# Four heads a step in the first mLSTM cell, and the second cell beside attention: a four-layer fp32 kernel on one Trainium2 core

## The chip, the cores and the metric

The kernel runs on one core of one Trainium2 chip. The metric is the device time of one execution in microseconds, the median over several runs. All arithmetic that matters here is in fp32.

## What is computed

Eight sequences b of 512 tokens and 256 features pass through four residual layers. The change touches the first layer and the entry to the second.

```python
x = x + tanh(g_xattn[0]) * mLSTM(layernorm(x), ctx, ctx)     # cell, 8 heads of 32
x = x + tanh(g_ffn[0])   * L0_ffn(layernorm(x))              # 32 heads of 8, then experts
x = x + tanh(g_xattn[1]) * cross_attention(ctx, ctx, layernorm(x))   # 16 heads of 16
x = x + tanh(g_ffn[1])   * key_value_memory(layernorm(x))

# mLSTM of one sequence, q = layernorm(x), k = v = ctx
log_f = log_sigmoid(fg); cs = cumsum(log_f)
log_D = where(causal, cs[:, None] - cs[None, :], -inf) + ig[None, :]
D = exp(log_D - max(log_D, -1))
C = (q k^T / sqrt(32)) * D
h = C / (max(|sum C|, exp(-max log_D)) + 1e-6) @ v
return layernorm(h) * ln_scale

# L0_ffn starts with a layer norm of its own: xn = layernorm(layernorm(x)) * ln_g + ln_b
```

## The kernel before

**Stages.** One long phase (`attention_phase`) holds the first three layers for all eight sequences; two shorter phases do the last layer. Sequences are taken in the order 0, 4, 1, 5, 2, 6, 3, 7 and numbered m = 0 to 7 in it. The backbone of the long phase is a list of 24 attention jobs: A(m, 0) and A(m, 1), the two halves of the heads of the second layer, and C(m, 0), the cross attention. Each job has 16 steps, each of two halves. Attention makes two passes: `maxima` (L397) multiplies queries with keys (L388, TensorE) and takes row maxima (L406, VectorE); after a job's last step `close_maxima` (L412) writes the maxima into the query operand; `exponentials` (L426) multiplies again and exponentiates (L434, ScalarE), and `values` (L440) sums with the values (L449). The two passes of neighbouring jobs run in the same steps: while one job exponentiates, the next one takes maxima.

**Work beside attention.** All else is written as Python generators, called lanes (L1147 to L1149): `before` runs `cell` and `queries`; `between` spreads operands and marks jobs ready; `behind` runs the experts and the operands of the cross attention; `after` and `fill` lead to the last layer. A lane yields a number, the TensorE time in rough microseconds that it has just used, or a tuple: `("wait", t)` asks not to be called before planned time t has gone by, `("rest", key)` waits for a key, `("take", on)` takes or gives back one PSUM bank that lanes share. After each half step `beside` (L1152) calls lanes until a credit of 1.1 or 2.1 units is used up. TensorE executes in exactly that written order; the order of the other engines is settled by a scheduler from the order of writing. A tick is one turn of the main loop (L1177): one step of the maxima of one job, of the exponentials of another, or both. Where no job is ready, ticks go by with lanes alone.

**The cell (L586 to L750), before.** For one sequence: x and the context are loaded by GpSimd's queue (L589, L497, L592), x is normalised, transposed to features (L313), and multiplied with the gate weights (L606). Gate functions on 8 partitions follow (L611 to L631), and the row of negated maxima goes to DRAM (L633), from where each of four pairs of heads reads it as a broadcast (L654). For a pair and each of four chunks of 128 keys: GpSimd masks the triangle (L662), ScalarE makes the decay of both heads (L670), TensorE the scores (L699), VectorE their product (L704), TensorE the sums with the keys (L677, 64 columns a head). Chunk c covers the queries from 128c on, so it has 512, 384, 256 or 128 columns. After the chunks the sums are transposed and divided (L715 to L737). At the end the result is normalised, scaled and added to x (L742 to L748).

**Two places for cells.** Class `Tiles` (L518) has buffers of its own; class `Lent` (L545) has its in those of the experts' weights, which come into use later. Sequences 0, 2, 4, 5, 6, 7 go through `Tiles`, 1 and 3 through `Lent`. Both lanes begin at once, so cells 0 and 1 run together ahead of attention. `queries` (L753) takes two layer norms one after the other (L755, L756), transposes, and projects to queries, keys and values through DRAM. `begin` (L801) spreads them over the attention operands: three sets `qa`, `ka`, filled by GpSimd at the start (L275, L276) and given rows of ones by SP (L284). The loop also holds back the exponentials of any job until the values of sequence 1 are made (L1189). `behind` waits for the end of the `Lent` lane.

## Time and profile before

| what | value |
|---|---|
| median of 3 runs | 3959.41 us (3946.13 to 3970.28) |
| the profiled execution | 3974.63 us, its span 3972.8 us |
| TensorE (PE) busy | 3616.3 us, 91% of the span |
| VectorE (DVE), ScalarE (ACT), GpSimd (POOL) busy | 57%, 44%, 16% |
| mean granted TensorE clock | 0.949 of full speed |
| maxima of the first job A(0, 0), L406 | 195.6 to 313.5 us |
| exponentials, L434, first and last | 327.7 us, 3054.3 us |

The profiled execution is one run, and 15 us longer than the median. Times in the profile count from the start of its span. A line such as `L388 PE MATMUL sc<-ka,qa` names the code line, the engine, the operation, and the tiles written and read. PE is TensorE's matmul row and PEld its weight loads; a busy PE is not PE at its peak. In the timeline an arrow in brackets names what ended the idle time of the engine before the instruction. The granted clock is that of TensorE alone. Each fp32 matmul appears as two instructions in the counts.

### The profile page before, as it was taken

The page shows a single profiled execution, that of the slowest core. Times are in us where ns is not written, and L with a number is a line of the kernel's source. Part 1 is how long each engine was busy: PE and PEld are TensorE (multiplying, and loading weights), DVE is VectorE, ACT ScalarE, POOL GpSimd, SP SyncE. Part 2 cuts the span into 40 slices and gives each one's busy share as a digit, 9 for nine tenths or more (in the row PEclk, how much of TensorE's full clock was granted, in tenths as well). Part 3 has the DMA queues.
Part 4 walks back from the last instruction along what each step waited for, and adds up shares of the span by engine and source line. Part 5 has one row for each costly group of instructions (what it writes and reads, how often), then busy time and mean ns, then how long its engine had stood idle before and what let it go on. Part 6 is the DMA issues. An engine that isn't in the chain of part 4 may idle for free.

```text
span 3972.8 us, 76203 instructions
## 1 busy us (share of the span) xinstructions
PE 3616.3 (91%) x31049; PEld 1861.4 (47%) x31049; DVE 2277.6 (57%) x5591; ACT 1763.3 (44%) x2305; POOL 617.2 (16%) x653
## 2 busy tenths in 40 slices
PE   5788889888899999999989988988899899999998
PEld 2332334333334433444434433434344677777776
DVE  4465665656555555554454453454421589999993
ACT  2213444454445445444444444434244355555552
POOL 3301121103001200200100010010000133333331
PEclk7567999999999999999999999999899999999999
DMA  3221221213222421333323223120333443333331
GB/s 95 93 74 38 72 73 58 86 39 81 77 73 76 117 75 57 100 95 91 95 80 105 80 64 97 60 71 25 120 107 120 112 130 103 104 103 112 111 108 36
DMA packets 221754, 339.05 MB, mean 85 GB/s; under 512 B 25998, under 2 KB 170926, under 8 KB 213102
## 3 DMA queue, kind: packets, MB, share of 16 engines
q1 hardware_dynamic: 203772, 273.04, 23.0%
q0 software_dynamic: 16768, 60.83, 5.3%
q8 instruction: 244, 4.00, 0.4%
q14 instruction: 106, 0.87, 0.1%
q10 hardware_dynamic: 864, 0.32, 0.0%
HBM read 236.66 MB, written 96.63 MB: 84 GB/s over the span
## 4 chain that ended last, share of the span: by engine, by line
PE 63%; DVE 8%; DMA 1%; ACT 1%; issue 1%; POOL 0%; SPq 0%; DVEq 0%; ACTq 0%; POOLq 0%
PE sc L388 17%; PE acc L1563 11%; PE ps_hd L131 10%; DVE nm L406 6%; PE av L449 5%; PE cf L1543 3%; PE ps_sim L1295 3%; PE ps_y L870 2%; PE ps_q L348 2%; PE ps_h L851 2%; PE ps_p L337 2%; PE ps_hl L131 1%; PE ps_g L964 1%; PE ps_t L318 1%; PE ot L470 1%
## 5 line engine op out<-in xcount | busy, mean ns | idle before, releaser
L406 DVE TENSOR_REDUCE nm<-sc 128x2 f32<-128x1024 f32 x768 | 940.4, 1225 | 1049.0 <-PE sc L388 1048.3
L434 ACT ACTIVATE pr<-sc 128x1024 f32<-128x1024 f32 x768 | 786.1, 1024 | 1009.9 <-PE sc L388 1009.4
L388 PE MATMUL sc<-ka,qa 32*128 32x512 f32 x3072 | 958.8, 673 | 162.5 <-DVE nm L406 141.4
L388 PE MATMUL sc<-qa,ka 32*128 32x512 f32 x3072 | 898.7, 658 | 19.4 <-ACT pr L434 17.1
L388 PEld LDWEIGHTS sc<-ka,qa 32*128 32x128 f32 x3072 | 260.6, 191 | 557.8 <-DVE nm L406 345.2
L1563 PE MATMUL acc<-up_sb,gs 64*128 64x256 f32 x4096 | 468.4, 382 | 1.3 <-DVE gs L1552 1.3
L131 PE MATMUL ps_hd<-xT,dw 128*64 128x256 f32 x3584 | 432.7, 387 | 9.1 <-DVE pd L704 5.0
L449 PE MATMUL av<-pr,v 128*32 128x512 f32 x3072 | 422.4, 623 | 1.1 <-ACT pr L434 1.1
L1563 PEld LDWEIGHTS acc<-up_sb,gs 64*128 64x128 f32 x4096 | 390.0, 187 | 52.3 <-issue 4.7
L131 PEld LDWEIGHTS ps_hd<-xT,dw 128*64 128x64 f32 x3584 | 243.6, 137 | 231.5 <-issue 100.9
L1533 POOL TENSOR_TENSOR m<-o,cwT 128x1024 f32<-128x1024 bf16 x128 | 243.7, 1904 | 562.9 <-DVE o L1531 240.7
L388 PEld LDWEIGHTS sc<-qa,ka 32*128 32x128 f32 x3072 | 242.5, 187 | 69.8 <-ACT pr L434 42.5
L1030 ACT COPY hb<-ps_hd 128x512 f32<-128x512 f32 x224 | 131.1, 586 | 307.8 <-PE ps_hd L131 283.6
L670 ACT ACTIVATE pd<-mb,aT 128x512 f32<-128x512 f32 (+3 forms) x256 | 128.9, 553 | 171.8 <-PE cav L677 89.0
L449 PEld LDWEIGHTS av<-pr,v 128*32 128x32 f32 x3072 | 61.4, 109 | 305.3 <-issue 289.7
L1552 DVE TENSOR_TENSOR gs<-cf,gs 128x1024 f32<-128x1024 f32 x128 | 155.6, 1217 | 42.2 <-PE cf L1543 27.4
L699 PE MATMUL csc<-qT,cT 32*128 32x384 f32 (+3 forms) x512 | 143.4, 580 | 13.8 <-DVE pd L704 7.4
L662 POOL TENSOR_SCALAR_AFFINE_SELECT mb<-mb 128x256 f32<-128x256 f32 x128 | 52.3, 409 | 653.3 <-ACT pd L670 370.6
L1543 PE MATMUL cf<-m,m 64*64 64x64 f32 x8192 | 152.4, 221 | 0.8 <-DVE gs L1552 0.7
L1543 PEld LDWEIGHTS cf<-m,m 64*64 64x64 f32 x8192 | 134.8, 135 | 38.7 <-issue 38.3
L704 DVE SCALAR_TENSOR_TENSOR pd<-csc,pd 128x512 f32<-128x512 f32 (+3 forms) x256 | 114.6, 483 | 66.4 <-PE csc L699 46.2
L1529 ACT CAST m<-o 128x1024 f32<-128x1024 bf16 x128 | 133.6, 1044 | 39.5 <-DVE o L1527 35.7
(232 smaller groups left out, 4134.6 us busy)
## 6 DMA issues: line engine op xcount, KB each, us to landing
h_d<-hb SPq DMA_DIRECT2D x224, 256.0 KB
gs<-h_d SPq DMA_DIRECT2D x56, 1024.0 KB
dw<-in_down SPq DMA_DIRECT2D x112, 256.0 KB
mb<-nM_d SPq DMA_DIRECT2D x32, 512.0 KB
qk_d<-pk SPq DMA_DIRECT2D x64, 256.0 KB
w1e<-in_w POOLq DMA_DIRECT2D x16, 1024.0 KB, 5.5
w2e<-in_w POOLq DMA_DIRECT2D x16, 1024.0 KB, 6.6
ws<-in_w SPq DMA_DIRECT2D x56, 256.0 KB
```

The lines of the kernel that those rows point to most:

```text
L131: nc.tensor.matmul(ps[64 * q : 64 * q + 64, :], dw[:, k, :], runs[:, :, q, :], start=(k == 0), stop=(k == NK - 1),)
L388: nc.tensor.matmul(sc[:, i, :], lhs[r : r + 32, g, c * P : (c + 1) * P], rhs[r : r + 32, g, :], start=True, stop=True,)
L406: newest = nc.vector.tensor_reduce(self.nm[:, c, 2 * half : 2 * half + 2, g], sc, AX.X, ALU.max, negate=True)
L434: nc.scalar.activation(self.pr[jj], sc, AF.Exp)
L449: nc.tensor.matmul(self.av[32 * j : 32 * j + 32, :], self.va[:, c, h * (self.hd + 1) : h * (self.hd + 1) + 32], pr[j // 2][:, j % 2, :], s ...
L699: nc.tensor.matmul(sc[i][:, s0:], cT[r : r + 32, g, s0 : s0 + P], qT[r : r + 32, g, s0:], start=True, stop=True,)
L1030: nc.scalar.copy(hb.rearrange("p n i t -> p i n t"), ps.rearrange("p i (n t) -> p i n t", n=2),)
L1529: nc.scalar.copy(m1, o1)
L1533: nc.gpsimd.tensor_tensor(m2, o2, tokens(cw), ALU.mult)
L1543: nc.tensor.matmul(cf[64 * q : 64 * q + 64, h, s, :], m2[rows, 4 * q + s // 2, :, s % 2], m1[rows, 4 * q + s // 2, :, s % 2], start=True, ...
L1552: nc.vector.tensor_tensor(gv, cf.rearrange("p h s i -> p i h s"), gv, ALU.mult)
L1563: nc.tensor.matmul(accs[n][q], gs[n % 2][rows, i, :], up_sb[rows, i, :], start=(i == 0), stop=(i == 63),)
```

## The change

- **Start.** x of the first sequence is loaded first, in two halves on SP's and ScalarE's queues, then its context and keys on SP's. GpSimd fills one set of attention operands at the start; `begin` has the other two filled when they are first wanted. The product of the output bias and the transposed mask (`constants`) come after the first cell's gate products.
- **First cell.** `all_pairs` does four heads in each of eight steps. Its broadcast rows lie in set 1 of the attention operands, half of its decays in set 2, its score products in the banks of the attention's scores. The decays run two steps ahead, the sums one step behind.
- **Its end.** The result's layer norm, scale and residual become two VectorE calls per chunk.
- **Layer norm of a layer norm.** For every sequence `queries` takes one statistic. With variance v it multiplies by 1/sqrt((1 + eps) v + eps^2), which is both norms in one.
- **Second cell.** `Tiles` takes sequences 0, 1, 3, 4, 5, 6, 7 and `Lent` takes 2 alone; it starts when the first attention job has started. The exponentials are not held for sequence 1 any more, and cells always share the one bank.

The diff, cut to its core; `close` holds what stood at L715 to L737.

```diff
-        for c in range(NC):
+        for c in range(NC) if dst is not None else ():
...
+        x0 = trp.tile([P, NC, D], F32, name="qn", tag="t1")
+        for c2 in range(2):
+            part = slice(2 * c2, 2 * c2 + 2)
+            (nc.sync, nc.scalar)[c2].dma_start(
+                x0[:, part], x[order[0]].rearrange("(c p) d -> p c d", p=P)[:, part]
+            )
...
+        cT0 = cxp.tile([P, NK, S], F32, name="cT", tag="cTc")
+        nc.sync.dma_start(cT0, cxT[order[0]].rearrange("(k p) s -> p k s", p=P))
+        cte = cst.tile([P, NC, WC], F32, name="cte")
+        nc.gpsimd.memset(cte, 1.0)
+        def load_keys(eng, ce, b):
+            for c in range(NC):
+                eng.dma_start(
+                    ce[:, c, : 8 * 33].rearrange("p (h e) -> p h e", e=33)[:, :, 0:32],
+                    cx[b, c * P : (c + 1) * P].rearrange("p (h e) -> p h e", e=32),
+                )
+        load_keys(nc.sync, cte, order[0])
...
+        def prepare(i):
+            qa, ka = sets[i]
             nc.gpsimd.memset(qa, 1.0)
             nc.gpsimd.memset(ka, 0.0)
-            sets.append((qa, ka))
+            if i:
+                give_ones(ka)
+        def give_ones(ka):
+            for j in range(4):
+                nc.sync.dma_start(
+                    ka[32 * j + 17 : 32 * j + 18, :, :], ones_d.rearrange("(o g) s -> o g s", o=1)
+                )
+        prepare(0)
         ones_d = drm.tile([4, S], F32, name="ones_d", bufs=1)
...
+        def constants():
...
+            def begin(self, m):
+                b = order[m]
+                if m == 0:
+                    return x0, cT0, cte
+                qn = self.tokens("qn")
+                nc.gpsimd.dma_start(qn, x[b].rearrange("(c p) d -> p c d", p=P))
+                cT, ce = self.context(m)
+                load_keys(nc.gpsimd, ce, b)
+                return qn, cT, ce
...
+        def all_pairs(qT, cT, ce, nM_d, aT, close):
+            room = [t[:, 2 * i : 2 * i + 2] for t in sets[1] for i in range(2)]
+            for pair in range(4):
+                nc.sync.dma_start(
+                    room[pair], nM_d[2 * pair : 2 * pair + 2].partition_broadcast(P)
+                )
+            spare = [t[:, 2 * i : 2 * i + 2] for t in sets[2] for i in range(2)]
+            pds, avs = {}, {}
+            steps = [(g, c) for g in range(2) for c in range(NC)]
+            def decay(n):
+                g, c = steps[n]
+                s0 = c * P
+                for pair in (2 * g, 2 * g + 1):
+                    mb = room[pair]
+                    nc.gpsimd.affine_select(
+                        out=mb[:, :, s0 : s0 + P], in_=mb[:, :, s0 : s0 + P],
+                        pattern=[[0, 2], [1, P]], compare_op=ALU.is_ge,
+                        fill=NEG, base=0, channel_multiplier=-1,
+                    )
+                    pd = pds[pair, c] = (
+                        spare[c - 1 + pair % 2] if c % 2
+                        else prb.tile([P, 2, S], F32, name="pr", tag="pr")
+                    )
+                    for i in range(2):
+                        h = 2 * pair + i
+                        nc.scalar.activation(
+                            pd[:, i, s0:], mb[:, i, s0:], AF.Exp, bias=aT[:, c, h : h + 1]
+                        )
+            def weigh(n):
+                g, c = steps[n]
+                s0 = c * P
+                two = {
+                    pair: ps_sc.tile([P, 2, S], F32, name="sc", tag="sc")
+                    for pair in (2 * g, 2 * g + 1)
+                }
+                for pair, sc in two.items():
+                    for i in range(2):
+                        r = 32 * (2 * (pair % 2) + i)
+                        nc.tensor.matmul(
+                            sc[:, i, s0:], cT[r : r + 32, g, s0 : s0 + P], qT[r : r + 32, g, s0:],
+                            start=True, stop=True,
+                        )
+                for pair, sc in two.items():
+                    pd = pds[pair, c]
+                    nc.vector.scalar_tensor_tensor(
+                        pd[:, :, s0:], sc[:, :, s0:], 1.0 / math.sqrt(32.0), pd[:, :, s0:],
+                        ALU.mult, ALU.mult,
+                    )
+            def sums(n):
+                g, c = steps[n]
+                for pair in (2 * g, 2 * g + 1):
+                    if c == 0:
+                        avs[pair] = (
+                            ps_av.tile([P, S], F32, name="av", tag="av") if pair % 2
+                            else ps_ac.tile([P, S], F32, name="cav", tag="ac")
+                        )
+                    for i in range(2):
+                        h = 2 * pair + i
+                        nc.tensor.matmul(
+                            avs[pair][64 * i : 64 * i + 64, c * P :],
+                            ce[:, c, 33 * h : 33 * h + 64],
+                            pds[pair, c][:, i, c * P :], start=(c == 0), stop=(c == NC - 1),
+                        )
+            decay(0)
+            decay(1)
+            for n in range(len(steps) + 1):
+                if n < len(steps):
+                    weigh(n)
+                if n > 0:
+                    sums(n - 1)
+                    g, c = steps[n - 1]
+                    if c == NC - 1:
+                        for pair in (2 * g, 2 * g + 1):
+                            close(pair, avs[pair])
+                if n + 2 < len(steps):
+                    decay(n + 2)
...
-            qn = own.tokens("qn")
-            nc.gpsimd.dma_start(qn, x[b].rearrange("(c p) d -> p c d", p=P))
-            cT, ce = own.context(m)
-            for c in range(NC):
-                nc.gpsimd.dma_start(
-                    ce[:, c, : 8 * 33].rearrange("p (h e) -> p h e", e=33)[:, :, 0:32],
-                    cx[b, c * P : (c + 1) * P].rearrange("p (h e) -> p h e", e=32),
-                )
+            qn, cT, ce = own.begin(m)
             yield ("wait", 4)
...
+            if m == 0:
+                constants()
...
+            def close(pair, av):
+                avs = trp.tile([P, S], F32, name="avs", tag="pk", bufs=2)
+                nc.any.tensor_copy(avs, av)
...
+            if m == 0:
+                all_pairs(qT, cT, ce, nM_d, aT, close)
+            for pair in range(4) if m else ():
...
-                def banks():
-                    if newest:
-                        return [ps_m.tile([P, S], F32, name="csc", tag="m") for _ in range(2)]
-                    two = ps_sc.tile([P, 2, S], F32, name="csc2", tag="sc")
-                    return [two[:, i] for i in range(2)]
...
+            if m == 0:
+                mu, rs = yield from layernorm(None, hk, "q")
+                for c in range(NC):
+                    nc.vector.scalar_tensor_tensor(
+                        hk[:, c, :], hk[:, c, :], mu[:, c, 0:1], lns, ALU.subtract, ALU.mult
+                    )
+                    nc.vector.scalar_tensor_tensor(
+                        Xa[:, c, :], hk[:, c, :], rs[:, c : c + 1], Xa[:, c, :], ALU.mult, ALU.add
+                    )
+            else:
+                yield from layernorm(hk, hk, "q" + own.user)
+                nc.gpsimd.tensor_tensor(
+                    hk, hk, lns.unsqueeze(1).to_broadcast([P, NC, D]), ALU.mult
+                )
+                nc.gpsimd.tensor_tensor(Xa, Xa, hk, ALU.add)
             xds[m] = drm.tile([P, NC, D], F32, name="x_d1", bufs=M)
...
-            lnx[m] = yield from layernorm(xn, Xa, "q" + own.user, kept=m)
-            yield from layernorm(xn, xn, "q" + own.user)
+            mu, rs = lnx[m] = yield from layernorm(None, Xa, "q" + own.user, kept=m)
+            both = small.tile([P, NC], F32, name="rs2", tag=f"rs2{own.user}", bufs=1)
+            nc.gpsimd.tensor_scalar(
+                both, mu[:, :, 1], 1.0 + EPS_LN, EPS_LN * EPS_LN, ALU.mult, ALU.add
+            )
+            nc.gpsimd.tensor_tensor(both, both, mhalf.to_broadcast([P, NC]), ALU.pow)
+            yield ("wait", 2)
+            for c in range(NC):
+                nc.vector.tensor_scalar(
+                    xn[:, c, :], Xa[:, c, :], mu[:, c, 0:1], both[:, c : c + 1],
+                    ALU.subtract, ALU.mult,
+                )
+                if c % 2:
+                    yield ("wait", 1.5)
...
+                if last is None and i:
+                    prepare(i)
...
+                if m == f == 0:
+                    yield ("wait", 6)
...
+            if tiles is Lent:
+                yield ("rest", ("begun", 0))
...
-        lanes += [Lane(before((0, 2, *range(4, M)), Tiles)), Lane(behind()), Lane(before((1, 3), Lent))]
+        lanes += [Lane(before((0, 1, *range(3, M)), Tiles)), Lane(behind()), Lane(before((2,), Lent))]
...
-                    or not free or ("v_d", 1) not in rested
+                    or not free
...
+                rested.add(("begun", 0))
```

## The prediction

> **What bounds the kernel now.** I read the page's slices first.
>
> ```profile
> PE   5788889888899999999989988988899899999998
> ...
> PEclk7567999999999999999999999999899999999999
> ```
>
> TensorE is at 8 or 9 tenths from the third slice (99 us each) to the end, at full clock from the fifth. What is left lies at the start: idle time, and a clock of 0.5 to 0.7 over four slices. Next, busy time by stretch (columns: length, then PE, PEld, DVE, ACT, POOL with counts, granted clock, DMA share, GB/s), and the matmuls of the maxima and the exponentials in the first 400 us.
>
> ```profile
> 0.00:60.00 60.00, 19.33 (x61) 9.07 (x61) 31.80 (x56) 12.54 (x17) 32.80 (x43) 0.90 0.44 116
> 60.00:192.60 132.60, 99.59 (x328) 43.16 (x328) 57.84 (x167) 36.64 (x75) 41.15 (x65) 0.54 0.28 88
> 192.60:327.00 134.40, 119.62 (x335) 44.88 (x338) 74.60 (x124) 27.12 (x50) 10.93 (x25) 0.61 0.22 56
> ...
> 800.70:921.30 120.60, 108.96 (x661) 46.66 (x664) 69.60 (x110) 61.01 (x77) 8.82 (x17) 0.99 0.16 43
> 921.30:1022.60 101.30, 86.22 (x540) 36.17 (x536) 63.86 (x116) 42.28 (x49) 30.64 (x36) 0.97 0.32 88
> ```
>
> ```profile
> L388 PE MATMUL sc<-ka,qa x204: 587/1056/1217, 192.7 to 397.2; 32*128 32x512 f32 x102
> ...
> L434 ACT ACTIVATE pr<-sc x17: 999/1024/1025, 327.7 to 397.9; 128x1024 f32<-128x1024 f32 x17
> ```
>
> No attention matmul runs before 192.7 us; the first exponential comes at 327.7. Until then two cells run together. Last, the timeline of that start (start, length, engine):
>
> ```profile
> 3.92 11.25 DVE L213 COPY gwm<-gw_sb 128x16 f32<-128x16 f32 x1 [2.92 <-DMA gw_sb<-in_gw]
> ...
> 20.39 1.41 DVE L98 BATCH_NORM_STATS2 ln_st<-qn 128x6 f32<-128x256 f32 x4 [3.90 <-DMA qn<-in_x]
> ...
> 31.86 0.73 DVE L107 TENSOR_SCALAR qn<-qn,ln_mv,ln_rs 128x256 f32<-128x256 f32 x2 [2.23 <-POOL ln_rs L104]
> ...
> 56.45 1.31 SPq L633 DMA_DIRECT2D nM_d<-pd  x2
> ...
> 62.08 0.42 POOL L662 TENSOR_SCALAR_AFFINE_SELECT mb<-mb 128x256 f32<-128x256 f32 x1 [23.14 <-DMA mb<-nM_d]
> ...
> 97.32 3.36 PE L699 MATMUL csc<-qT,cT 32*128 32x512 f32 x8
> ...
> 100.61 2.15 PE L677 MATMUL cav<-pd,cte 128*64 128x512 f32 x4
> ...
> 149.95 0.32 SPq L748 DMA_DIRECT2D x_d<-Xa  x1
> ...
> 171.90 0.73 DVE L107 TENSOR_SCALAR xn<-xn,ln_mv,ln_rs 128x256 f32<-128x256 f32 x2 [0.58 <-POOL ln_rs L104]
> ```
>
> The chain of cell 0 is latency up to 62 us, matmul at half clock to about 140, and layer norms and projections from there to 192.7.
>
> **What the Trainium skill says.** "SBUF — State Buffer", Who interferes with whom: a VectorE copy in a two-port mode and a GpSimd instruction share a port pair that one holds whole while the other blocks. The trace agrees: a 16-element copy lasts 11.25 us, from 3.92 until the GpSimd fills end at 15.1, and everything on VectorE queues behind it. "TensorE: Matmul & The Clock Gate", Part 1: the clock is at half after an idle window and at full after a busy one. The trace agrees on the two values, yet shows 0.54 over 60 to 192.6 although PE is busy 99.6 of 132.6 us; so I price the start at both clocks. Same page, Part 3: matmuls of 32 rows in four different row groups run side by side. The attention products here use it; the old cell used two groups.
>
> **The change, part by part: the path to the first maximum.**
>
> Loads and fills. x goes out first on SP's and ACT's queues, and nothing of the second cell. It should land by about 6 us, but VectorE is held by the GpSimd fills until those end: ident 0.5, gwm 0.24, cell keys 1.08, one set of attention operands instead of three (2 x 1.80), v0 1.25, v1 1.05: 7.7 from 0.7, so 8.5. Statistics 1.41 and 0.36, rs on GpSimd about 1.5 with its hand-overs: the first normalised chunk at 12.2 instead of 31.9. GpSimd no longer issues 2 x 5.3 us of loads ahead of rs. SP gets about seven more issues of 0.4 us and a wait for the key fill ahead of the weights, which are wanted 80 us later: no cost. I allow 8 to 16.
>
> Gates. From first chunk to the row of maxima took 24.6 us (31.9 to 56.45) for two cells interleaved. Without the other cell's gate matmuls (3.4) and its exponents and scans in between (about 3) it is 18: 30 (28 to 34). The moved constants (bo product 2.1 us of PE, 1.2 of VectorE) lie under ScalarE's gate functions; at worst 1 us. Write and broadcast took 5.6 (56.45 to 62.08): 36. Four broadcasts of 512 KB now compete, so up to 4 more.
>
> All pairs. Per group of four heads at half clock: scores side by side 2.08, 1.65, 1.22, 0.80 by chunk, 5.75; sums 2.15, 1.55, 1.12, 0.70 per pair, 11.0 for two; transposes 2.2. Two groups: 38. At full clock 19. ScalarE needs 2 x 4 x (0.66 + 0.56 + 0.46 + 0.35) = 16.3, VectorE 12.8 (one call per pair for two; the old calls of 0.65, 0.53, 0.41, 0.28 would make 15, one start of 0.16 less each, about 12.8) plus 4.8 of divisions: 17.6. With 8 of lead-in and last division: 46 at half clock; at full clock about 30, as steps alternate between PE and VectorE. I take 38: 74.
>
> Norms. The cell's own norm and residual took 10 us (139.9 to 149.95), with two GpSimd calls of 2.34 each. Now statistics 1.8, rs 1.5, eight VectorE calls of about 0.45: 7. The double norm took 22 (149.95 to 171.9); now one statistic, four small GpSimd calls (2 x 0.23 + 2 x 1.04) and hand-overs: 4. From the normalised chunk to the first maximum 20.8 (171.9 to 192.7), unchanged. 74 + 7 + 4 + 20.8 = 106. **Gain 192.7 - 106 = 87** (bounds 53 with everything late at 140, 103 at 90).
>
> **What comes back.** Cell 1 now runs beside attention. Its yields add up to 2.2 (features) + 3.6 (gates) + 0.8 + 4 x 6.325 (pairs) = 31.9 units, in a planner that hands out 1.1 + 2.1 = 3.2 a tick. Counting lanes tick by tick by the code's own yields, old and new order both take 412 ticks from the first maximum to the last sum; the loop does 29 units more, nearly all in ticks that had spare credit (job A(2,0) 43 units for 33, A(5,1) 52 for 43, A(6,1) 35 for 26). A unit's price: the job of 800.7 carries 52 units and takes 120.6 us, that of 921.3 carries 29 and takes 101.3: 0.84; against the job of 693.6 (33 units, 107.1 us) 0.71. 29 x 0.75 = **22 us** (15 if spare time hides half, 32 at 1 us a unit).
>
> Cell 1's operands are ready at tick 29 by that count, wanted at 32: no stall, margin three ticks. The fills of sets 1 and 2 (7.2 us of GpSimd) and their eight small stores move behind the first maximum; their jobs start 16 and 32 ticks later, so nothing waits; at worst 4 us if they get ahead of a store on SP, which all stores of the features share. The double norm saves 3.5 us of VectorE per sequence; VectorE is at 57%: nothing. The dropped test on the second cell's values bound nothing: it was done at 269, the exponentials began at 327.7. The first 32 ticks keep their length: maxima plus about as much beside them (43 and 34 units for 42 and 44).
>
> **Sum.** -87 + 22 = -65. The profiled execution took 3974.6 (span 3972.8 plus 1.8), so its like would take 3910; it lies 15 above the median 3959.4, and against that I predict **3895**.
>
> **Rivals.** *A slow start* (chance 0.15): PE stays at half clock, broadcasts queue, VectorE is held longer; so that its early x gains little; the first maximum at 140. For it: 0.54 granted, and the 43 us that GpSimd waited for broadcasts. Against: nothing is queued beside cell 0 now. 3959 - 53 + 22 = 3928. *The work of cell 1 is free* (0.12): spare credit and idle PE time hide it and the start runs at full clock; first maximum at 95, 5 us back: 3959 - 98 + 5 = 3866. *PE blocks behind the cells* (0.05): PE keeps its program order, so a score or sum of cells 1 and 2 that waits for GpSimd, ScalarE and VectorE holds the attention products behind it. There are 2 x 4 x 4 = 32 such chunks in the first 32 ticks; the gain of 65 is gone at 2.0 us each, and at 3.0 the result is 3959 - 65 + 96 = 3990. Against: cells 2 and 3 stood in the same place before, and PE was busy 119.6 of 134.4 us.
>
> **Numbers.** The forecast 0.68. Differences under 0.5% (20 us) cannot be told from no change here. Range: from the lowest own case (first maximum 90, 15 back: 3871) and the free case 3866 less some scatter, to the slow start plus scatter: 3856 to 3938. Faster by over 0.5%: the forecast, the free case and most of the slow start, 0.89; within 0.06; slower 0.05.
>
> **What would show it.** First maximum at 100 to 112 us, first exponential 130 to 140 after it, first broadcast select near 36, eight-matmul score steps, maxima of A(1,0) directly behind A(0,1), last exponential near 2990. Wrong if the first maximum is after 130, if A(1,0) stalls, or if the attention stretch (2728 us from first to last exponential) grows by over 35.

## The result

The changed kernel takes 3934.7 us (median of 12 runs, 3929.6 to 3947.3) where the kernel before, beside it on the same chips, takes 3967.6: the ratio is 0.9931, with a 95% interval of 0.9914 to 0.9949. It is 33 us faster. The forecast was a change of 65; the time lies inside the stated range, but half of the expected gain is missing. The profiled execution took 3939.58 us, 35 less than that of before.

### The profile after

First the slices of the page, TensorE's busy time and its granted clock.

```profile
PE   4898899898999999889999989988899999999998
...
PEclk7658999999999999999999999999899999999999
```

The rows of the kernel before began with `5788` and `7567`. TensorE is busier in the second slice now (98 to 197 us), but the clock is still low in slices 2 and 3 (0.6 and 0.5). Next, the tile of the attention's scores up to 420 us (durations in ns min/median/max, then first and last start).

```profile
L417 PE MATMUL sc<-ka,qa x298: 587/692/1218, 113.9 to 417.3; 32*128 32x512 f32 x149
...
L463 ACT ACTIVATE pr<-sc x40: 1001/1024/1026, 266.7 to 419.2; 128x1024 f32<-128x1024 f32 x40
```

The first attention product starts at 113.9 instead of 192.7: 78.8 us earlier. The first exponential starts at 266.7 instead of 327.7: only 61 us earlier. So 18 us are lost within the first job. The last exponential ends at 3020.9 instead of 3055.3, 34 earlier. The timeline of the start shows where the 113.9 comes from (start, length, engine).

```profile
5.59 1.41 DVE L98 BATCH_NORM_STATS2 ln_st<-qn 128x6 f32<-128x256 f32 x4 [4.59 <-DMA qn<-in_x]
...
7.11 1.04 POOL L315 MEMSET v<- 128x1148 f32 x1
8.13 0.23 POOL L103 TENSOR_SCALAR ln_rs<-ln_mv 128x4 f32<-128x4 f32 x1
...
9.37 1.06 POOL L104 TENSOR_TENSOR ln_rs<-ln_rs,eps 128x4 f32<-128x4 f32 x1
...
15.69 0.63 SPq L319 DMA_DIRECT2D m_u<-in_mask  x1
...
27.17 0.21 DVE L321 CAST m_f<-m_u 32x128 f32<-32x128 uint8 x1 [15.24 <-DMA m_u<-in_mask]
27.31 1.36 DVE L107 TENSOR_SCALAR qn<-qn,ln_mv,ln_rs 128x256 f32<-128x256 f32 x4
...
44.74 0.27 SPq L739 DMA_DIRECT2D nM_d<-pd  x1
...
50.20 0.42 POOL L631 TENSOR_SCALAR_AFFINE_SELECT qa<-qa 128x256 f32<-128x256 f32 x1 [10.29 <-DMA qa<-nM_d]
...
81.96 1.41 DVE L98 BATCH_NORM_STATS2 ln_st<-hk 128x6 f32<-128x256 f32 x4
...
92.14 1.38 DVE L880 TENSOR_SCALAR xn<-Xa,ln_mv,rs 128x256 f32<-128x256 f32 x4 [2.73 <-POOL rs L877]
...
113.89 6.57 PE L417 MATMUL sc<-ka,qa 32*128 32x512 f32 x12 [3.19 <-issue]
```

x is there at 5.6 us and its rs at 10.4, as hoped. But the normalised chunk waits until 27.3: ahead of it in VectorE's order of instructions stands the cast of the mask. The bracket says what that cast waited for, 15.24 us long: its load. SP issued that load at 15.69, behind the context, the keys and three loads of weights. In the kernel before it had gone out at 4.94:

```profile
4.94 0.46 SPq L301 DMA_DIRECT2D m_u<-in_mask  x1
```

Then two views of the first job (maxima of A(0, 0)). By stretch: length, then busy time of PE, PEld, DVE, ACT and POOL, granted clock, DMA share, GB/s. The first line is the job in the kernel before, the others are of the changed one.

```profile
195.60:313.50 117.90, 105.38 (x300) 40.58 (x300) 67.76 (x115) 21.29 (x42) 10.37 (x23) 0.62 0.24 62
```

```profile
117.10:254.20 137.10, 123.00 (x335) 41.27 (x332) 75.48 (x129) 35.72 (x65) 12.12 (x28) 0.56 0.15 40
160.00:252.00 92.00, 86.75 (x236) 30.94 (x238) 47.48 (x82) 24.72 (x49) 8.66 (x21) 0.50 0.11 38
254.20:383.40 129.20, 108.30 (x559) 38.11 (x559) 73.39 (x142) 46.16 (x66) 30.27 (x41) 0.83 0.25 77
```

From 160 to 252 us (the second of these three lines) the clock is at half without a break, though PE is busy 86.75 of 92 us. PE's products of this job by shape, first in the kernel before (195.6 to 313.5 us, 118 long), then in the changed one (117.1 to 254.2, 137 long):

```profile
L388 PE MATMUL sc<-ka,qa 32*128 32x512 f32 x124 | 49.8, 992 | 2.6 <-DVE nm L406 2.6
L348 PE MATMUL ps_q<-ws,nT 128*128 128x256 f32 x24 | 11.5, 628 | 3.6 <-DVE pd L704 3.1 <-DMA ws<-in_w 0.5
L337 PE MATMUL ps_p<-nT,ws 128*128 128x256 f32 x32 | 8.0, 392 | 1.2 <-DVE pk L770 0.8 <-DVE nT L322 0.4
...
L677 PE MATMUL cav<-pd,cte 128*64 128x512 f32 x8 | 4.0, 1088 | 0.0
...
L699 PE MATMUL csc<-qT,cT 32*128 32x512 f32 x8 | 3.5, 761 | 0.0
```

```profile
L417 PE MATMUL sc<-ka,qa 32*128 32x512 f32 x123 | 59.6, 1010 | 2.3 <-DVE nm L435 2.2
L826 PE MATMUL csc<-qT,cT 32*128 32x512 f32 x20 | 17.4, 1081 | 1.8 <-ACT em L751 1.8
L826 PE MATMUL csc<-qT,cT 32*128 32x384 f32 x20 | 15.5, 890 | 0.1
L811 PE MATMUL cav<-pd,cte 128*64 128x512 f32 x20 | 9.9, 1088 | 0.0
```

The old job carried the projections of a sequence and little of a cell; the new one has no projection, but more than twice as many of the cells' scores (32 to 76 instructions) and sums (32 to 72). These rows count products that run side by side twice. Counted from the trace, with the products in the order of their ends, as the time that each adds after the end of the one before it, the job of before has 9.4 us of `csc`, 10.1 of `cav` and 18.9 of projections; that of after has 33.4, 23.0 and none. The difference, 36.9 - 18.9 = 18, is the growth of PE's busy time (105.4 to 123.0), and nearly that of the job (19.2). (Ordered by their starts, the cells' scores get 5 us less of the later job and the attention's 5 more; the total is the same.)

Last, the way of the lead after that: the stretches from the first maximum of the first job to that of the fifth, and on to that of the twentieth, in the kernel before and in the changed one.

```profile
195.60:693.60 498.00, 436.45 (x2164) 173.25 (x2168) 297.28 (x537) 192.72 (x271) 80.26 (x123) 0.84 0.22 62
693.60:2348.80 1655.20, 1526.71 (x10136) 663.00 (x10132) 882.40 (x1299) 760.77 (x914) 183.92 (x250) 0.98 0.28 82
```

```profile
117.10:613.30 496.20, 440.80 (x2127) 167.53 (x2128) 283.26 (x484) 196.52 (x276) 79.57 (x124) 0.82 0.22 64
613.30:2315.50 1702.20, 1576.61 (x10332) 686.57 (x10328) 910.08 (x1360) 777.00 (x947) 206.41 (x280) 0.98 0.29 82
```

The lead is 78.5 us at the first maximum, 80.3 at that of the fifth job, 33.3 at that of the twentieth, and 34.4 at the end of the exponentials. So the first job's loss is made good by the third and fourth job. The first four jobs hold equally many of the cells' products in both kernels (192 score and 192 sum instructions), though the changed one leaves 28 products of the experts, about 9 us, to later jobs. Jobs 5 to 19 then hold 256 and 256 where they held 192 and 192, one cell more, and take 47 us longer.

### The profile page after: what moved, and what is told of

Read it like the earlier page. It is cut to its first block, busy times and chain, and to the rows that moved or that the text cites. A ratio compares the mean times of both kernels' runs of the same rounds, so it can differ in the third digit from the quotient of the medians.

```text
span 3937.6 us, 76092 instructions
## 1 busy us (share of the span) xinstructions
PE 3599.6 (91%) x31049; PEld 1853.6 (47%) x31049; DVE 2244.4 (57%) x5483; ACT 1760.8 (45%) x2304; POOL 608.9 (15%) x645
## 4 chain that ended last, share of the span: by engine, by line
PE 78%; DVE 11%; issue 3%; ACT 3%; DMA 2%; POOL 1%; SPq 0%; DVEq 0%; POOLq 0%; ACTq 0%
PE sc L417 22%; PE acc L1699 12%; PE ps_hd L131 10%; DVE nm L435 7%; PE av L478 7%; PE cf L1679 4%; PE ps_y L1003 3%; PE ps_sim L1431 3%; PE ps_p L366 3%; PE ps_q L377 3%; PE ps_h L984 3%; PE csc L826 2%; PE cav L811 1%; PE ps_hl L131 1%; PE ps_t L347 1%
## 5 line engine op out<-in xcount | busy, mean ns | idle before, releaser
L417 PE MATMUL sc<-ka,qa 32*128 32x512 f32 x3072 | 974.1, 672 | 138.6 <-DVE nm L435 119.8
L131 PE MATMUL ps_hd<-xT,dw 128*64 128x256 f32 x3584 | 430.5, 386 | 10.2 <-DVE pd L831 5.8
L804 ACT ACTIVATE pd<-mb,aT 128x256 f32<-128x256 f32 (+2 forms) x224 | 113.1, 553 | 184.8 <-PE cav L811 100.6
L1688 DVE TENSOR_TENSOR gs<-cf,gs 128x1024 f32<-128x1024 f32 x128 | 155.8, 1219 | 42.4 <-PE cf L1679 27.3
L826 PE MATMUL csc<-qT,cT 32*128 32x512 f32 (+1 forms) x448 | 136.2, 537 | 12.3 <-DVE o L506 5.0
L984 PE MATMUL ps_h<-fT,w1e 128*128 128x256 f32 x512 | 133.7, 397 | 5.4 <-DVE o L506 4.8
```

The source lines that it names most:

```text
L131: nc.tensor.matmul(ps[64 * q : 64 * q + 64, :], dw[:, k, :], runs[:, :, q, :], start=(k == 0), stop=(k == NK - 1),)
L417: nc.tensor.matmul(sc[:, i, :], lhs[r : r + 32, g, c * P : (c + 1) * P], rhs[r : r + 32, g, :], start=True, stop=True,)
L826: nc.tensor.matmul(sc[i][:, s0:], cT[r : r + 32, g, s0 : s0 + P], qT[r : r + 32, g, s0:], start=True, stop=True,)
L984: nc.tensor.matmul(ps[:, :D], w1e[:, k, f * P : (f + 1) * P], fT[:, k, i * D : (i + 1) * D], start=(k == 0), stop=(k == NK - 1),)
L1688: nc.vector.tensor_tensor(gv, cf.rearrange("p h s i -> p i h s"), gv, ALU.mult)
```

## The experiments

Each kernel ran beside the kernel before on its chip; its ratio is to that. The changed kernel's ratio is 0.9931. All edits are to the changed kernel. "First product" is the first attention matmul (113.9), "first job" the maxima of A(0, 0) (137.1 us long).

### The start

**The mask's load early.**

```diff
+        m_u8 = cst.tile([B * NC, P], U8, name="m_u8")
+        nc.sync.dma_start(m_u8, mask)
         cT0 = cxp.tile([P, NK, S], F32, name="cT", tag="cTc")
...
-        m_u8 = cst.tile([B * NC, P], U8, name="m_u8")
-        nc.sync.dma_start(m_u8, mask)
         m_f = trp.tile([B * NC, P], F32, name="m_f", tag="pk", bufs=2)
...
             yield 0.9
-            if m == 0:
-                constants()
...
             yield 0.8
+            if m == 0:
+                constants()
```

> The mask's load of 4 KB goes out ahead of the context's, and the constants come after the transposes of the gate rows. Held by the mask: the first normalised chunk comes at about 12 us instead of 27.3, the first maximum at about 99 instead of 113.9, and the time falls by about 15 us below the changed kernel (3935 to 3920, ratio to before 0.988). If that wait was covered by something else that is as late (gate bias, weights of the gates), the first chunk stays after 22 us and the time stays within 5 us of 3935.

3921.1 us, ratio 0.9892 (0.9865 to 0.9919). The start of its timeline:

```profile
4.17 0.32 SPq L217 DMA_DIRECT2D m_u<-in_mask  x1
...
7.23 1.00 DVE L321 CAST m_f<-m_u 32x128 f32<-32x128 uint8 x1
...
10.10 1.51 DVE L277 TENSOR_SCALAR lns<-lns,tg 128x256 f32<-128x256 f32 x1 [1.87 <-DMA lns<-in_ln_scale]
...
11.86 1.51 DVE L107 TENSOR_SCALAR qn<-qn,ln_mv,ln_rs 128x256 f32<-128x256 f32 x4
```

From issue to cast it is 3 us instead of 11.5, the first chunk comes at 11.9, and the first product at 99.6. These 14 us stay through all later jobs (14 to 21 in the trace). The edit also moves the constants behind the transposes of the gate rows, but that gains nothing: from the first chunk to the row of maxima it is 17.8 us here and 17.4 in the changed kernel. The wait for the mask was real, and 14 us is its price.

**The first sequence's loads back on GpSimd's queue.**

```diff
-        for c2 in range(2):
-            part = slice(2 * c2, 2 * c2 + 2)
-            (nc.sync, nc.scalar)[c2].dma_start(
-                x0[:, part], x[order[0]].rearrange("(c p) d -> p c d", p=P)[:, part]
-            )
...
-        nc.sync.dma_start(cT0, cxT[order[0]].rearrange("(k p) s -> p k s", p=P))
...
-        load_keys(nc.sync, cte, order[0])
...
                 if m == 0:
+                    nc.gpsimd.dma_start(x0, x[b].rearrange("(c p) d -> p c d", p=P))
+                    nc.gpsimd.dma_start(cT0, cxT[b].rearrange("(k p) s -> p k s", p=P))
+                    load_keys(nc.gpsimd, cte, b)
                     return x0, cT0, cte
```

> The first sequence's transfers go back to GpSimd's queue behind its fills. Theory that the mask hid their early arrival: x is there at about 20 us, before the mask's cast lets go at 27, so the time stays within 5 us of 3935. By the forecast's reading (x is what the start waits for) the first maximum comes about 10 us later and the time with it, 3945.

3933.2 us, ratio 0.9925 (0.9897 to 0.9952): not to be told from the changed kernel. In the trace x comes later, but the chunk 8 us earlier, and the first product 7.5 (106.4):

```profile
11.36 0.30 DVE L314 CAST m_f<-m_u 32x128 f32<-32x128 uint8 x1 [3.06 <-DMA m_u<-in_mask]
...
15.12 1.41 DVE L98 BATCH_NORM_STATS2 ln_st<-qn 128x6 f32<-128x256 f32 x4 [3.22 <-DMA qn<-in_x]
...
19.02 2.19 DVE L107 TENSOR_SCALAR qn<-qn,ln_mv,ln_rs 128x256 f32<-128x256 f32 x4 [2.22 <-POOL ln_rs L104]
```

"Its transfers first" as built is worth nothing: it takes back with the mask at least what it gives with x. That it costs 7 us, as the trace has it, is too little for these medians to show.

**Pairs one after another in the first cell.**

```diff
-            if m == 0:
-                all_pairs(qT, cT, ce, nM_d, aT, close)
-            for pair in range(4) if m else ():
+            for pair in range(4):
```

> The first cell goes pair by pair like the others. Its four pairs at half clock and one broadcast place took about 12 us a pair for each of two interleaved cells before; alone 15 to 18 each with the wait for the broadcast: 60 to 72 us where the four-head steps took 32 (50 to 82 us). The first maximum comes 28 to 40 us later, and the time with it: 3963 to 3975, no better than before the change. If the work beside attention absorbs the delay: under 3950.

3961.7 us, ratio 0.9989 (0.9968 to 1.0010): the whole gain is gone, 27 us by the medians. The first product starts at 135.4, 21.5 later, and the first job is as long as with the change (137.4). (The two traces are only 13 us apart at their ends.)

**Two layer norms in the queries.**

```diff
-            mu, rs = lnx[m] = yield from layernorm(None, Xa, "q" + own.user, kept=m)
...
-                if c % 2:
-                    yield ("wait", 1.5)
+            lnx[m] = yield from layernorm(xn, Xa, "q" + own.user, kept=m)
+            yield from layernorm(xn, xn, "q" + own.user)
```

> The layer norm of a layer norm is done in two again. The forecast gave 22 us for cell 0's two norms in the kernel before and 4 in the changed one; that cell had the second cell beside it, and a norm alone took 6 to 7 us here. So the first maximum should come 6 to 10 us later; the later sequences' norms lie beside attention and cost nothing. 3940 to 3946. If VectorE were short in the later jobs, eight more norms of 3.5 us would add up to 28 us: 3970.

3933.1 us, ratio 0.9917 (0.9891 to 0.9944): no difference. The first product starts at 116.1, 2.2 later. The one step needs a pow on GpSimd twice, one behind the other, and so takes 4.4 us (87.7 to 92.1) where two norms take 7.6 (86.1 to 93.7). The 22 us that they took before were mostly the second cell's work in between. In the trace of before, the second norm's pow waits on GpSimd behind two calls of that cell:

```profile
166.02 2.35 POOL L743 TENSOR_TENSOR hk<-hk,lns 128x1024 f32<-128x1024 f32 x1
...
168.53 2.34 POOL L746 TENSOR_TENSOR mb<-mb,hk 128x1024 f32<-128x1024 f32 x1
170.82 1.04 POOL L104 TENSOR_TENSOR ln_rs<-ln_rs,eps 128x4 f32<-128x4 f32 x1
```

### The second cell beside attention

**The second cell ahead.** The first job waits until the second cell's values are made.

```diff
                 if m == f == 0:
-                    yield ("wait", 6)
+                    yield ("rest", ("v_d", 1))
```

> The first attention job waits until the second cell's queries, keys and values are made; the rest of the change stays. This undoes only 'the second cell beside attention'. Theory (the units cost the same wherever they are done, those under the half clock more): the first maximum 75 to 110 us later, near 200, the first job about 105 instead of 137, and 27 to 40 us returned afterwards; 3970 to 3990, that is, at or above the kernel before. If the second cell beside attention were worth nothing, since all of its work comes back, the time would stay at 3935. The forecast's own price (0.75 us a unit) gives 3935 + 100 - 22, about 4013.

4006.6 us, ratio 1.0107 (1.0082 to 1.0133), 72 us over the changed kernel and slower than the kernel before.

```profile
L417 PE MATMUL sc<-ka,qa x192: 587/1052/1218, 219.1 to 419.7; 32*128 32x512 f32 x192
```

The first product starts 105 us later; of these, 33 (by the medians) to 42 (by the traces) come back. Both parts are about what I wrote (75 to 110 and 27 to 40), but the total that I put to them, 3970 to 3990, took only the low end of the delay; it was missed. So was the first job: 126.4 us instead of 105, for without the second cell the later cells moved up into it (72 of their score instructions and 64 of their sums, against 76 and 72). Together with the run that does the first cell's pairs one after another, this says something the forecast did not: neither half of the change helps alone. Four heads a step with the cells one after the other is slower than before. The old kernel ran its two cells interleaved, which may be why; no run tests that. The second cell beside attention with the old first cell gives nothing.

**The third cell only after the first job.**

```diff
             if tiles is Lent:
-                yield ("rest", ("begun", 0))
+                yield ("rest", ("closed", 0))
...
                     closed[one[0]] = tick
+                    if one[0] == jobs[0]:
+                        rested.add(("closed", 0))
```

> The lane of cell 2 starts when the maxima of the first job are closed, not when they start. Theory of the half clock (two cells beside maxima alone are dear, because TensorE runs at half clock there): the first job's maxima take about 100 us instead of 137, the work of cell 2 is done later at full clock for about 25, and the time falls by 10 to 20 us to about 3920. Theory of units alone (a unit costs the same wherever it is done): the job is shorter by as much as later jobs are longer, 3935 within 6. If the operands of A(2,0) come late: longer, over 3945.

3941.6 us, ratio 0.9937 (0.9917 to 0.9957): no gain. The first job shrinks by 33 us to 104.2, the third grows by 31 to 139.8 and the fourth by 9 to 122.9. The third job now holds the cells' products, 104 instructions of `csc` and 108 of `cav` instead of 48 and 48, and its clock is 0.82 instead of 0.94:

```profile
356.00:495.90 139.90, 123.51 (x643) 39.08 (x635) 81.41 (x166) 58.64 (x87) 25.89 (x42) 0.82 0.18 52
```

**All cells in one lane.**

```diff
-Lane(before((0, 1, *range(3, M)), Tiles)), Lane(behind()), Lane(before((2,), Lent))
+Lane(before(range(M), Tiles)), Lane(behind()), Lane(before((), Lent))
```

> All eight cells go through one lane, so that no two cells run at the same time; the lent place stays empty. Theory of crowding (two cells at once keep TensorE at half clock, and their score and sum products then cost about 0.42 and 0.32 us each instead of 0.18 and 0.17): the first job's maxima fall from 137 to about 105 us as in the run where cell 2 came later, no later job rises over 125, and the time falls by 20 to 35 us to about 3907. Theory of units (the same work costs the same wherever it stands): first job shorter, later jobs longer by as much, 3935 within 8. If sequence 2 comes late for A(2,0): longer.

3943.8 us, ratio 0.9952 (0.9935 to 0.9968). The first job takes 103.3 us, the second 87.8. At its end the run is 63 us ahead of the changed kernel in the trace, after the fifteenth job 45, and after the nineteenth, A(6, 1), 10: its cells are done later, up to the eighteenth job, where the changed kernel has none after the fifteenth. So the crowding of the two lanes is not what costs: moved to later jobs, the same work brought no gain.

**Extra products to keep PE busy.** 96 products that nobody reads are added to the first job.

```diff
+                if one and not two and one[0] == jobs[0]:
+                    for _ in range(3):
+                        nc.tensor.matmul(warm, hot[:, :P], hot, start=True, stop=True)
                 for _, then in work:
                     then()
```

> While the first job's maxima run alone, each half step gets three bf16 matmuls of 128 rows and 512 columns more, whose result nobody reads: 96 in all, 0.21 us each at full clock, 20 us. Theory of the half clock (the thin products of the cells and of the maxima alone do not keep the clock up): the share of full clock in the job rises from 0.13 to over 0.7 and the job gets shorter in spite of more work, 137 to about 105, time about 3905. If the clock there has another cause (it stays at half): the job grows by 30 to 40 us, time about 3970. If the job waits for the cells' chains and not for TensorE: within 10 of 137.

3970.4 us, ratio 1.0004 (0.9987 to 1.0021): they cost 36 us and lift nothing. The clock over the first job:

```profile
117.00:286.00 169.00, 159.05 (x427) 47.39 (x427) 79.17 (x132) 32.87 (x57) 12.35 (x28) 0.58 0.12 33
```

PE is busy 94% of the time, at 0.58 of full clock.

**Maxima in four row groups.** Where a job's maxima run without exponentials, both halves of a step are issued together, four products in four row groups.

```diff
+                alone = one and not two
-                if one:
-                    work.append(live[one[0]].maxima(one[1], half))
+                for part in (half,) if not alone else (0, 1) if half == 0 else ():
+                    if one:
+                        work.append(live[one[0]].maxima(one[1], part))
```

> Where maxima run without exponentials, the four products of a step go out together in four row groups, before both reductions. Theory of the half clock: the products of the first job, 49 us of TensorE's time between 113 and 266 us, take about half, the job falls from 137 to about 112 us, the time by 15 to 30 us to about 3912. If the chain of the two cells sets the length of that stretch, not TensorE's time: the job stays within 8 us of 137 and the time within 8 of 3935.

3922.5 us, ratio 0.9890 (0.9862 to 0.9919), 12 us better than the changed kernel. The first job takes 123.0 us, not the 112 hoped for.

```profile
L417 PE MATMUL sc<-ka,qa 32*128 32x512 f32 x121 | 42.7, 1014 | 5.4 <-DVE nm L435 5.4
```

A product is as long as before (1014 ns), but the row's busy time falls from 59.6 to 42.7: more of them run side by side.

### What the second cell's pairs cost

**Left out, later work moving up.**

```diff
-            for pair in range(4) if m else ():
+            if m == 1:
+                nc.gpsimd.memset(hk, 1.0)
+            for pair in range(4) if m > 1 else ():
```

> Leaves out the four pairs of heads of the second sequence (its cell result is a constant), 25.3 units. The forecast's price of 0.75 us a unit: 19 us less, 3916. A full price of 0.96: 24 less, 3911. Theory of the half clock (work beside maxima alone costs 1.5 to 2 us a unit): 38 to 50 less, 3885 to 3897, and the first job's maxima take about 100 us instead of 137.

3892.1 us, ratio 0.9816 (0.9787 to 0.9845): 42.6 us for 25.3 units, 1.68 a unit. The first job takes 110.8.

**The same pairs twice in the sixth sequence.**

```diff
-            for pair in range(4) if m else ():
+            for pair in (*range(4), *(range(4) if m == 5 else ())) if m else ():
```

> The four pairs of the sixth sequence's cell (m = 5) are done twice, with the same outcome: 25.3 units more in the middle of the kernel, where PE runs at full clock. Leaving the same work out of the second sequence's cell gave 42.6 us (1.68 a unit). If that price was high because this work lay under the half clock, the price here is that of the middle: 0.75 (the forecast's) to 0.96 (the displaced work's) a unit, 19 to 25 us, 3954 to 3960. If every unit costs 1.7 us wherever it lies, 43 us: 3977.

3949.8 us, ratio 0.9964 (0.9947 to 0.9980): 15 us by the medians, 13 by the ratios, 0.5 to 0.6 a unit. It is less than either theory said. So taking out and adding differ by three, and two things differ with them: the place, and what the planner does with other work. The next two runs hold the order fixed.

**Left out with its turns kept, in the second cell and in the sixth sequence's.** The diff is that of the second cell; the other has 5 for 1.

```diff
+            if m == 1:
+                nc.gpsimd.memset(hk, 1.0)
+                for pair in range(4):
+                    yield ("wait", 2.5)
+                    yield ("wait", 1.5)
+                    yield ("take", True)
+                    for c in range(NC):
+                        yield 1.1 * (NC - c) / NC + (1.1 * (NC + 1 - c) / NC if c else 0)
+                        yield ("wait", 1.5)
+                    yield ("take", False)
+                    yield 1.1
-            for pair in range(4) if m else ():
+            for pair in range(4) if m not in (0, 1) else ():
```

> Leaves out the four pairs of the second cell (its result is set to one), but keeps every one of their turns in the planner, so that all other work stays in its place; the run that left the pairs out altogether let other work move up. In the first job of the changed kernel PE gave 0.42 us to each score product's half and 0.32 to each sum's, beyond the products already running: 64 of each make 27 and 20, so 47 us less if all lie in the first job and nothing else limits it; 40 allows for a third of the sums in the second job at a better clock. Theory (these products are dear in the first job): 3890 to 3898, the first job 100 to 110. Forecast's price (0.75 a unit, 25.3 units): 3916.

> The same edit in the sixth sequence's cell (m = 5), in the middle of the kernel: the same 25.3 units, the same turns, PE at full clock. Theory: 0.185 and 0.17 us for each half product, as in the job of 385 to 497, 64 of each: 23 us, 3912. If a unit of these pairs costs the same wherever it lies, this run and the one that hollows out the second cell fall together. If the middle has room that hides them, under 10 us: 3925 or more.

The second cell: 3887.9 us, ratio 0.9801 (0.9780 to 0.9821), 47 us by the medians and 52 by the ratios. Its first two jobs take 104.3 and 100.3 us instead of 137.1 and 127.1, and from there to the end every job is 49 to 55 us earlier. The sixth sequence's cell: 3911.2 us, ratio 0.9855 (0.9837 to 0.9872), 23 by the medians and 30 by the ratios; the trace has 28 in the two jobs where that work lay (and gives 8 of them back in the last job, at a clock of 0.85). The same 25.3 units cost 1.9 to 2.0 us each in the first jobs, and 0.9 to 1.2 in the middle. The place sets the price. Yet the two runs that moved cells out of the first job gained nothing; why work that is left out there saves so much and work that is moved from there saves none, these runs do not separate. The clock of the first job without the second cell's pairs:

```profile
123.00:227.30 104.30, 83.87 (x247) 27.57 (x243) 64.09 (x98) 23.42 (x39) 8.83 (x18) 0.57 0.17 43
```

It is still near half: the second cell's pairs pay for the low clock there, they do not make it alone. In the second job the clock rises without them, from 0.83 to 0.93.

**VectorE's product left out of the second cell.**

```diff
-                    for i in range(2):
+                    for i in range(2 if m != 1 else 0):
                         nc.vector.scalar_tensor_tensor(
                             pds[c][:, i, s0:], sc[i][:, s0:], 1.0 / math.sqrt(32.0),
                             pds[c][:, i, s0:], ALU.mult, ALU.mult,
                         )
```

> In the second cell alone VectorE's multiplication of scores and decays is left out; its sums take the decays as they are, and all matmuls stay. If the first job is longer because PE waits in its order for VectorE (the rival of the forecast that priced a chunk's wait), 32 chunks are freed of it: 15 us or more, and the first job under 125. If the products themselves are the cost, as the theory has it, only the idle time put down to these multiplications goes (7.9 us), so 5 to 10: 3925 to 3930, first job 128 to 133.

3936.5 us, ratio 0.9918 (0.9902 to 0.9933): nothing; the first job takes 135.9. VectorE is relieved of 8.5 us in it (75.48 to 66.98 busy) and PE's 123 us stay at 122. Even the small saving I expected is not there. PE's products are the cost, not its waits between them. Nor can waits for GpSimd or ScalarE be: PE is idle for 14.1 us of the changed first job and was for 12.5 of the old one.

### The best version

The early mask and the four row groups together.

> The early mask and the maxima in four row groups, both at once. They act in different places (the first 27 us; the first job), so they should add: 13.5 and 12 us on top of the changed kernel, about 3909 where the changed kernel has 3935; the first maximum near 103 and the first job's maxima 123 us long. If the first job is limited by the clock alone, a start 14 us earlier changes nothing in it. If the two share one slack (a job that waits for the second cell's operands), the sum falls short and the time stays near 3921.

3914.1 us, ratio 0.9869 (0.9845 to 0.9893): 1.3% below the kernel before and 21 us below the changed one, where some 26 would be the full sum. In the trace both parts are there whole: first product at 99.1, first job 123.0 us long, 28 us earlier at its end.

## Why the forecast was wrong

**The loads.** "SP gets about seven more issues of 0.4 us [...] ahead of the weights, which are wanted 80 us later: no cost" failed. I looked at who needs the weights and not at the mask, whose load went behind the same issues and whose cast stands in VectorE's order ahead of the first chunk. First chunk 27.3 instead of 12.2. The step before it, VectorE held by the fills to 8.5 us, gave nearly the right number by luck: with the mask early the chunk came at 11.9. But VectorE's statistics began at 5.6, as soon as x was there and with fills still running. The fills held GpSimd's own part of the norm instead (to 8.1), and VectorE then waited until 10.1 for the load of the layer norm's scale, and scaled it and copied the gate weights ahead of the chunk.

**The path to the first product.** Gates 17.4 us (forecast 18), write and broadcast 5.5 (5.6; little queueing of the four broadcasts), all pairs 31.8 (38, between my values of 46 and 30 for half and full clock; the clock there was 0.77), norms 10.2 (11), projections to the first product 21.8 (20.8). Sum 113.9 against 106: the mask's 15 too many and the pairs' 6 too few make most of these 8. The gain was 78.8, not 87. The single norm was given 18 of these; by itself it is worth 2. That does not touch the sum, since the 22 us of before were really gone, but the reason that I gave was wrong: the second cell had left.

**What comes back.** This is the step that failed most. I took 29 units at 0.75 us each, 22 us, and let "the first 32 ticks keep their length": I compared 43 and 34 units with 42 and 44 and took equal units for equal time. Measured, 44 us came back (78.8 at the first product, 34.4 at the last exponential), 1.5 us a unit. The first job grew from 118.0 to 137.1 us for one unit more, and the second kept its 127 for ten fewer. In the first job the units were now scores and sums of cells, before they were largely projections, and under the low clock 56.4 us of the former stand where 19.5 of them and 18.9 us of projections stood. The planner's yields price a pair at 6.3 units; in this place four pairs cost about 50 us, two a unit, where 0.75 a unit makes 19.

The third and fourth jobs made up for the first, and the lead was lost in jobs 5 to 19, where one cell more took 47 us. The price of 0.75 was too low there as well: the sixth sequence's pairs alone cost 23 to 30 us taken out (0.9 to 1.2 a unit), though only 13 to 15 put in a second time (0.5 to 0.6). How the rest of the 47 divides between the cell's gates and norms and the experts' products moved there, no run shows.

**The sum.** 78.8 - 44.4 = 34.4, and the two profiled executions differ by 35; the forecast had 87 - 22 = 65. So 8 of the missing 30 us lie before the first product and 22 in what comes back. The second figure rests on one trace of each kernel: from the second job's first maximum to the end of the exponentials, five runs with the same work there (the changed kernel and those with the early mask, the extra products, the later x, and the pairs one after another) took 2754 to 2769 us. That the time lies in the stated range, near the 3928 of the rival "slow start", is that rival's merit only in part: VectorE was held longer and the early x gained little, but by the load of the mask, and its first maximum at 140 and its queue of broadcasts did not come. That the second cell's work is free is refuted.

**What held.** A(1, 0) follows A(0, 1) without a stall (383.4 to 384.9). The rival of PE waiting behind the cells' VectorE products is refuted by the run without them. The stretch from first to last exponential grew by 27, short of the 35 that I had set as the mark of a failure, so none of the three marks of a failure was met. A mark on that stretch does not see the job ahead of its first exponential, where 18 us of the lead had gone by then. The sign that did show it was the first exponential, 153 us after the first product and not 130 to 140.

**What stays open** is why the clock is at half. "TensorE: Matmul & The Clock Gate" of the Trainium skill, Part 1, has the clock released by a busy window. Here the measurement decides otherwise: 86.75 us busy of 92 at 0.50, and 159 of 169 at 0.58 with products added. In the first job, where maxima run without exponentials, it is low in every run (0.55 to 0.64). Later it is low in some jobs with many of the cells' products (0.82 with 212 of them, in the run with the third cell late), but not in all (0.99 with 116, in the sixth job of the kernel before), and once in a job with none (0.85, the last job of the run without the sixth sequence's pairs). No run separates the cause.

## What to carry to other kernels

When loads are put at the head of a queue, list what is pushed back on it, and look on the consuming engine for any instruction, however small, that waits for one of these ahead of the critical work; a 0.2 us cast cost 14 us. A planner's unit is not a time: before work is moved, price it in its new place by the shape of its products and the clock granted there. A shorter head of a kernel is worth what is left after the work taken out of it has been paid for elsewhere; here 79 us became 35.

## What the hardware showed beyond that

A 4 KB load takes at most 3 us when it is issued early (4.17 to the cast at 7.23), and 11.5 us behind the context, keys and weights (15.69 to 27.17). The granted clock can stay at half for 92 us while PE is busy 94% of the time.
